# Patch projection, scan sums and gating products of a two-image Mamba-style block moved between engines

## Chip, cores and metric

The kernel runs on one NeuronCore of a Trainium2 chip, in one launch, in float32. The metric is the device time of one execution in microseconds (us), taken as the median of three runs. The engines are named as in the profile: PE is TensorE (the matrix engine), DVE is VectorE, ACT is ScalarE, POOL is GpSimd and SP is SyncE, which here only issues DMAs. PEld is the loading of weights into PE. PE writes to PSUM, a small memory beside the large SBUF.

## What is computed

Two images of 128 channels and 64 x 64 pixels pass two MetaFormer layers. Each layer has a token mixer and a mixture-of-experts network:

```
layer 0 mixer : four deformable convolutions (1x1, 1x1, 3x3, 7x7), a pooled branch, 1x1 fusion
layer 0 MLP   : top-2 of 8 experts
layer 1 mixer : h = LayerNorm(x); in_proj 128 -> 512 channels; depthwise 5x5 convolution
                x half (256): channel attention, causal conv1d of 4 taps, SiLU
                z half (256): position attention, SiLU
                dt = softplus(...); state[n] = exp(dt*A[n])*state[n] + dt*x*B[n]   (n = 0..15)
                y = (sum over n of C[n]*state[n] + D*x) * silu(z); out_proj 256 -> 128; residual
layer 1 MLP   : mixture of 64 experts
```

The change is in the layer 1 mixer. Its two matrix parts are linear, so the input projection may be done before or while the image is cut into patches, and the sum over n may be made in either orientation of the matrix.

## The kernel before

The order of every engine's instructions is written out by hand (`manual_schedule`). The long stages run in turn. Work that can go beside a stage is written as Python generators that yield; a `Side` object advances them by `step()`, so many steps per turn of the stage's loop. The order in which the Python program emits instructions is the order of each engine's queue.

1. **Sampling** (`L0Conv.sample`, L535): for each image, 8 groups of 60 taps, 480 turns of the loop. A turn gathers 4 x 128 rows of 2 KB by four indirect DMAs of POOL (L547), weights them on DVE (L558, L563, L564), transposes them on PE (L568), copies them on ACT (L577) and multiplies them on PE (L597). During the sampling of image 2, `rest` holds everything that image 1 needs up to its scan (`after(0)`: `finish`, the first MLP and `L1Conv.convs`). It is stepped 3 times per turn in the first group and 2 times in the others (L526).
2. **Scan** (`L1Conv.scan`, L1221): the sequence of each image is cut into 8 pieces of 512 positions. Of each piece there are 32 units: 16 states n by 2 halves of 128 channels; 512 units in all. A unit u is
   - POOL: `drive(u + 3)`, the product db = du * B of three units later (L1246)
   - ACT: the copy of the last unit's end state (L1310), then `decay(u + 2)`, da = exp(A*dt) into PSUM (L1253)
   - DVE: the scan, in place in da in PSUM (L1303), then the C product sc = da * C into SBUF (L1313)
   - PE: `add` of the last unit's sc to the accumulators py by four 128 x 128 identity transposes (L1271)
   - `side.step()` twice, which advances `prepare` of the next piece (L1118) and `project` of the last one (L1333)
   - during image 1, `rest.step()` five times, which advances `after(1)`, the same work for image 2 as in stage 1 for image 1.

   The rows of B and C are loaded, broadcast to 128 partitions, into `bcb`, 512 KB for each n, with 6 buffers (L1261). `rest` and `side` must be empty before the last units of a piece (L1292, L1305).
3. **Last MLP** (`L1Ffn.run`).

`L1Conv.convs` (L912) is where the patches are. `norm` (L1009) normalizes 512 tokens, transposes them and stores the normalized image `hd` to DRAM. Then, for each of four pairs of 64-channel blocks o, `strips` (L1024) loads `hd` again in 8 groups, projects it to 128 channels (one 128 x 128 by 512 matmul, L1032) and copies it by three ACT copies into `hs`, the image in overlapping strips. For each block o: 88 transposes cut 12 x 10 patches out of `hs` (L959) to give X; 64 matmuls with position matrices `tm` do the 5 x 5 convolution (L972) to give Y; and 48 transposes bring Y back to images of 64 channels (L988), stored by DMA. `copy` is an ACT copy of PSUM, `later` holds copies back by two steps. `channel_stats` and `channel_attention` follow block 3 and `position_attention` follows block 7.

`prepare` makes xs, zz (gated z), dt (`dl`), dt*x (`du`) and B, C (`bc`) of a piece, with a softplus polynomial whose first step is L1195 on DVE, and D*x (`dx`, L1217) on ACT. `project` copies py to SBUF (L1337), transposes it back (`pty`), multiplies it by zz (L1349), projects it (L1354), adds the residual and stores.

Of the kernel before, what the change touches and what calls it, by code (L numbers as in the profile page):

```python
# [176 lines left out]
class L0Conv:  # L177
# [279 lines left out]
    def run(self, build, after):  # L457
# [3 lines left out]
        with ExitStack() as ctx:  # L461
# [62 lines left out]
            for g in range(NG):  # L524
                nxt = self.load_group(1, g + 1) if g + 1 < NG else None
                self.sample(1, g, *cur, conv, rest, 2 if g else 3)  # L526
                cur = nxt
# [309 lines left out]
BCB = 6  # L837
# [31 lines left out]
class L1Conv:  # L869
# [3 lines left out]

    def __init__(self, env, dp, wp, x2, x3):
        nc, d = env.nc, env.d
        self.env, self.dp, self.x2, self.x3 = env, dp, x2, x3
        self.pos = dp.tile([512 // CG, KP, NPOS, CG], F32, name="pos")

        def load(name, shape, src=None):
            t = wp.tile(shape, F32, name="w_" + name)  # L880
            nc.sync.dma_start(out=t, in_=d[name] if src is None else src)
            return t

        self.wp = wp
        self.c1w = load("conv1d_w", [P, 2, 4])
        self.c1b = load("conv1d_b", [P, 2])
        self.xpw = load("x_proj_w", [P, 2, 40])
        self.dtb = load("dt_proj_b", [P, 2])
        self.A = load("A_log", [P, 2, DS])
        self.D = load("D", [P, 2])  # L890
        self.fc1 = load("ca_fc1_w", [P, 2, 16])
        self.fc2 = load("ca_fc2_w", [16, 256])
        self.saw = load("sa_conv_w", [14, 1])
        self.sqb = wp.tile([P, len(SQUARES)], F32, name="sqb")
        for i, (_, t, _) in enumerate(SQUARES):
            nc.vector.memset(self.sqb[:, i : i + 1], t)
        nc.scalar.activation(self.A, self.A, AF.Exp)
        nc.vector.tensor_scalar(self.A, self.A, -1.0, None, ALU.mult)
        self.xsd = [self.dp.tile([256, 3 + N], F32, name=f"xsd{b}", tag=f"xsd{b}") for b in range(B)]
        self.zsd = [self.dp.tile([256, N], F32, name=f"zsd{b}", tag=f"zsd{b}") for b in range(B)]  # L900
        self.hd = [self.dp.tile([P, N], F32, name=f"hd{b}", tag=f"hd{b}") for b in range(B)]
        self.att = [self.dp.tile([2, N + 6], F32, name=f"att{b}", tag=f"att{b}") for b in range(B)]
        self.sad = [self.dp.tile([1, N], F32, name=f"sad{b}", tag=f"sad{b}") for b in range(B)]
        self.w1 = [wp.tile([P, 2, 4], F32, name=f"w1_{b}") for b in range(B)]
        for b in range(B):
            for h in range(2):
                nc.sync.dma_start(out=self.xsd[b][h * P : (h + 1) * P, 0:3], in_=env.zero[:, 0:3])
            for s in range(2):
                nc.sync.dma_start(out=self.att[b][s : s + 1, 0:3], in_=env.zero[0:1, 0:3])
                nc.sync.dma_start(out=self.att[b][s : s + 1, N + 3 :], in_=env.zero[0:1, 0:3])  # L910

    def convs(self, b, sp, pp):  # L912
# [31 lines left out]
        yield from mixed([self.norm(b, g, sp, bank) for g in range(NG)], 2)  # L944
        zst = sp.tile([NPATCH, 2, 4, NPOS], F32, name="zst", bufs=1)
        for o in range(512 // CG):
            if o % 2 == 0:
                own = ipw[:, o * CG : (o + 2) * CG]
                yield from mixed([self.strips(b, g, own, hs, sp, bank) for g in range(NG)], 2)
# [4 lines left out]
            ch = slice(o % 2 * CG, (o % 2 + 1) * CG)  # L954
            for p0 in range(0, NPATCH, 8):
                ps = bank([KP, 8, CG], "ps1")
                for k in range(8):
                    i, j = divmod(p0 + k, NJ)
                    nc.tensor.transpose(  # L959
                        ps[:, k, :],  # L960
                        hs[ch, j, PH * i : PH * i + PH + 4, :].rearrange("p y x -> p (y x)"),
                        env.ident[ch, ch],
                    )
# [4 lines left out]
            Y = sp.tile([NPATCH, NPOS, CG], F32, name="Y", bufs=1)  # L968
            for c0 in range(0, CG, 8):
# [5 lines left out]
                later(copy(Y[:, :, c0 : c0 + 8], ps.rearrange("p c s -> p s c")))  # L975
                yield
            yield from last()

            x_half = o < 4
            for py in range(PH):  # L980
                img = sp.tile([CG, NI, W], F32, name="img", tag="io", bufs=3)
                ch = slice((o % 4) * CG, (o % 4 + 1) * CG)
                dst = self.xsd[b][ch, 3:] if x_half else self.zsd[b][ch, :]
                dst = dst.rearrange("c (i y x) -> c y i x", y=PH, x=W)[:, py, :, :]
                for x0, nx in ((0, 4), (4, 2)):
                    ps = bank([CG, nx, NPATCH], "ps3")
# [11 lines left out]
            if not x_half:  # L998
                nc.vector.tensor_reduce(zst[:, 0, o - 4, :], Y, AX.X, ALU.add)
                yield  # L1000
                nc.vector.tensor_reduce(zst[:, 1, o - 4, :], Y, AX.X, ALU.max)
# [7 lines left out]
    def norm(self, b, g, sp, bank):  # L1009
# [10 lines left out]
        nc.scalar.copy(hn, pb)  # L1020
        nc.scalar.dma_start(out=self.hd[b][:, g * 512 : (g + 1) * 512], in_=hn.rearrange("p j t -> p (j t)"))
        yield

    def strips(self, b, g, own, hs, sp, bank):  # L1024

        nc = self.env.nc
        h = sp.tile([P, 512], F32, name="h", tag="io", bufs=3)
        nc.sync.dma_start(out=h, in_=self.hd[b][:, g * 512 : (g + 1) * 512])
        for _ in range(3):
            yield  # L1030
        pb = bank([P, 8, W], "pj")
        nc.tensor.matmul(pb.rearrange("p y x -> p (y x)"), own, h, start=True, stop=True)  # L1032
        yield
# [84 lines left out]
    def prepare(self, b, k, sp, pp, res):  # L1118
# [9 lines left out]
        zz = sp.tile([P, 2, LC], F32, name="zc")  # L1128
        nc.sync.dma_start(out=zz, in_=self.zsd[b].rearrange("(h p) l -> p h l", p=P)[:, :, l0 : l0 + LC])
        xr = sp.tile([P, GT, C], F32, name="xr")  # L1130
        nc.sync.dma_start(out=xr, in_=self.x2[b][:, k * GT : (k + 1) * GT, :])
        sa = sp.tile([P, LC], F32, name="sab", bufs=1)
        nc.sync.dma_start(out=sa, in_=self.sad[b][0, l0 : l0 + LC].partition_broadcast(P))
# [4 lines left out]
        yield from gap(6)  # L1138

# [55 lines left out]
        nc.vector.tensor_scalar(q, e, LINEAR[0], LINEAR[1], ALU.mult, ALU.add)  # L1195
# [19 lines left out]
        dx = sp.tile([P, 2, LC], F32, name="dx", bufs=1)  # L1215
        for h in halves:
            nc.scalar.mul(dx[:, h, :], xs[:, h, :], self.D[:, h : h + 1])  # L1217
        res.update(dx=dx, zz=zz, dl=dl, du=du, xr=xr)
        yield

    def scan(self, sp, ps, pp, rest, ahead):  # L1221
# [4 lines left out]
        for state in states:  # L1226
            nc.vector.memset(state, 0.0)
        NK = N // LC
# [10 lines left out]
        pieces, das, dbs, bcb, tail = {0: res}, {}, {}, {}, iter(())  # L1239
# [23 lines left out]
        adds, py = deque(), []  # L1263

        def add(half, what, first, last):

            if first:
                py.append(ps.tile([P, GT, P], F32, name=f"py{half}", tag=f"py{half}", bufs=1))
            out = py[half]
            for j in range(GT):  # L1270
                nc.tensor.matmul(  # L1271
                    out[:, j, :],
                    what[:, j * P : (j + 1) * P],
                    env.ident,
                    is_transpose=True,
                    start=first and j == 0,
                    stop=last and j == GT - 1,
                )
# [6 lines left out]
        side, keep = Side(), None  # L1285
        for u, (k, n, half) in enumerate(units):
            now, i, state = pieces[k], u // 2, states[k // NK]
            if n == 0 and half == 0:
                side.add(tail)
# [13 lines left out]
            nc.vector.tensor_tensor_scan(s, s, dbs.pop(u), state[:, half, n : n + 1], ALU.mult, ALU.add)  # L1303
# [8 lines left out]
            sc = sp.tile([P, LC], F32, name="sc", bufs=5)  # L1312
            nc.vector.tensor_tensor(sc, s, bc[:, 1, :], ALU.mult)  # L1313
            keep = state[:, half, n : n + 1], s[:, LC - 1 : LC]
            for _ in range(2 if rest.todo or k != NK - 1 else 4):
                side.step()
            for _ in range(5):
                rest.step()

            while adds:  # L1320
                add(*adds.popleft())
            if n == 0 and half == 0:
                py.clear()
                adds.extend((h, now["dx"][:, h, :], True, False) for h in range(2))
            adds.append((half, sc, False, n == DS - 1))
            if n == DS - 1 and half == 1:
                add(*adds.popleft())
                yt = sp.tile([P, 2, GT, P], F32, name="yt", bufs=1)
                tail = self.project(k // NK, k % NK, tuple(py), yt, now["zz"], now["xr"], pp)
        for _ in tail:  # L1330
            pass

    def project(self, b, k, py, yt, ys, xr, pp):  # L1333

        env, nc = self.env, self.env.nc
        for half in range(2):
            nc.scalar.copy(yt[:, half, :, :], py[half])  # L1337
        yield
        yield
        pts = []  # L1340
        for half in range(2):
            pt = pp.tile([P, GT, P], F32, name="pty", tag="m")
            transpose4(nc, env.ident, pt, [yt[:, half, j, :] for j in range(GT)])
            pts.append(pt)
            yield
        yield
        for half in range(2):
            y = ys[:, half, :]
            nc.vector.tensor_tensor(y, y, pts[half].rearrange("p j t -> p (j t)"), ALU.mult)  # L1349
            yield  # L1350
# [368 lines left out]
```

## Time and profile before

| what | us |
|---|---|
| median of three runs | 8280.49 (8272.83 to 8282.75) |
| the profiled execution's own time | 8332.4 |
| its span, first instruction to last | 8330.6 |
| PE, PEld busy in it | 5808.5, 4000.1 |
| DVE, ACT, POOL busy in it | 5729.7, 2120.9, 4590.5 |
| mean granted PE clock | 0.8 |

Read against the units' first and last instructions in the trace, the sampling of image 1 runs to 3150 us, that of image 2 to 6038 us, the first piece is prepared alone until 6085 us, the scan of image 1 runs to 7436 us, that of image 2 to 8055 us, and the last MLP to the end.

In the rows of the profile, "busy" is the time an engine's instructions of a group cover, then comes the mean of one in ns, then the idle time just before them and what ended it. In a table of windows the number after x counts instructions. A row of the timeline gives the start, the length, the engine, the line, what is written and read, and how many equal instructions were merged.

### The profile page before, as it was taken

The numbers are of one execution on the slowest core, as the hardware profiler recorded it, in microseconds if no ns is written. First come the engines' busy times: TensorE is split into PE (matmuls) and PEld (weight loads), VectorE is DVE, ScalarE is ACT, GpSimd is POOL, SyncE is SP. The second block draws the span as 40 slices with busy tenths as digits, with TensorE's granted clock in tenths as the row PEclk, the third lists the DMA queues.
The fourth block names the chain that finished last, engine by engine and source line by source line (L and its number), as shares of the span: only waits on it lengthen the run. The fifth ranks groups of instructions, "written<-read, shape, count | busy, mean of one in ns | idle before, by whom it ended". The sixth has DMA issues, their size and how long they took to land. (4 is left out here: it accounts for less than half of the span.)

```text
span 8330.6 us, 83751 instructions
## 1 busy us (share of the span) xinstructions
PE 5808.5 (70%) x27808; PEld 4000.1 (48%) x27808; DVE 5729.7 (69%) x8508; ACT 2120.9 (25%) x4432; POOL 4590.5 (55%) x4576
## 2 busy tenths in 40 slices
PE   2688888888888867766766676666755565855558
PEld 2456656666666644443434443344434444733335
DVE  1577777777777776777786667666647745669981
ACT  1111111111111113211111221112163344655540
POOL 0456666666666666666666666666534433347640
PEclk7788999999999988888888888788876665656568
DMA  4677666666666668867677777777653344434434
GB/s 128 185 249 216 195 207 203 205 213 197 207 203 206 208 212 261 270 213 234 218 240 203 228 204 223 219 206 216 176 166 135 127 110 107 128 106 149 145 124 141
DMA packets 636007, 1579.35 MB, mean 190 GB/s; under 512 B 167700, under 2 KB 247356, under 8 KB 623036
## 3 DMA queue, kind: packets, MB, share of 16 engines
q0 software_dynamic: 307200, 1006.88, 40.6%
q1 hardware_dynamic: 298284, 515.10, 19.5%
q10 hardware_dynamic: 30096, 52.03, 1.7%
q8 instruction: 226, 3.70, 0.2%
q14 instruction: 201, 1.65, 0.1%
HBM read 1456.11 MB, written 120.01 MB: 189 GB/s over the span
## 5 line engine op out<-in xcount | busy, mean ns | idle before, releaser
L547 POOL DMA_INDIRECT v<-table,idx x3840 | 3643.7, 949 | 2384.2 <-issue 1000.0
L597 PE MATMUL out<-st,regw 128*128 128x512 f32 x3840 | 2115.3, 676 | 161.2 <-issue 108.7
L558 DVE TENSOR_TENSOR v<-v,pw 128x1024 f32<-128x1024 f32 x960 | 1169.5, 1218 | 1060.9 <-DMA v<-table,idx 871.0
L568 PE MATMUL pst<-ident,v 128*128 128x128 f32 x7680 | 1240.2, 304 | 823.3 <-issue 529.5
L577 ACT COPY st<-pst 128x512 f32<-128x512 f32 x960 | 558.3, 585 | 4347.3 <-remote 2367.5
L568 PEld LDWEIGHTS pst<-ident,v 128*128 128x128 f32 x7680 | 1001.1, 157 | 1162.1 <-issue 786.9
L564 DVE TENSOR_TENSOR v<-v,low 128x512 f32<-128x512 f32 x1920 | 1318.0, 686 | 65.4
L563 DVE TENSOR_TENSOR low<-v,pw 128x512 f32<-128x512 f32 x1920 | 1329.0, 692 | 33.4
L1246 POOL TENSOR_TENSOR db<-du,bcb 128x512 f32<-128x512 f32 x512 | 660.0, 1293 | 937.2 <-DVE da L1303 897.4
L597 PEld LDWEIGHTS out<-st,regw 128*128 128x128 f32 x3840 | 762.0, 221 | 776.6 <-issue 713.7
L334 PEld LDWEIGHTS po<-wout,ring 128*128 128x128 f32 x5120 | 740.1, 198 | 366.5 <-issue 365.1
L334 PE MATMUL po<-wout,ring 128*128 128x147 f32 x5120 | 785.6, 299 | 167.4 <-issue 162.3
L1303 DVE TENSOR_TENSOR_SCAN da<-da,state,db 128x512 f32<-128x512 f32 x512 | 657.1, 1283 | 278.3 <-ACT da L1253 260.8
L1271 PE MATMUL py<-ident,sc 128*128 128x128 f32 x2048 | 463.0, 379 | 336.2 <-DVE sc L1313 335.1
L1271 PEld LDWEIGHTS py<-ident,sc 128*128 128x128 f32 x2048 | 338.6, 196 | 476.8 <-DVE sc L1313 441.5
L1313 DVE TENSOR_TENSOR sc<-da,bcb 128x512 f32<-128x512 f32 x512 | 354.2, 692 | 48.6 <-DVE da L1303 1.9
L1253 ACT ACTIVATE da<-delta,w_A_log 128x512 f32<-128x512 f32 x512 | 354.0, 692 | 17.3 <-DVE delta L1209 1.5
L972 PE MATMUL ps<-tm,X 120*88 120x48 f32 x2048 | 246.1, 299 | 62.9 <-ACT Y L924 22.5
L972 PEld LDWEIGHTS ps<-tm,X 120*88 120x88 f32 x2048 | 241.7, 213 | 94.4 <-issue 41.4
L959 PE MATMUL ps<-ident,hs 64*120 64x64 f32 x1408 | 142.1, 271 | 124.9 <-ACT X L924 69.8
L988 PE MATMUL ps<-ident,Y 88*64 88x88 f32 x768 | 108.1, 291 | 155.9 <-ACT img L924 100.1
L959 PEld LDWEIGHTS ps<-ident,hs 64*120 64x120 f32 x1408 | 125.5, 177 | 184.2 <-ACT X L924 89.5
(270 smaller groups left out, 4811.1 us busy)
## 6 DMA issues: line engine op xcount, KB each, us to landing
bcb<-bc SPq DMA_DIRECT2D x256, 512.0 KB
regw<-in_regw SPq DMA_DIRECT2D x66, 1280.0 KB
v<-table,idx POOLq DMA_INDIRECT x3840
yd<-ys ACTq DMA_DIRECT2D x128, 256.0 KB
yc<-yd SPq DMA_DIRECT2D x32, 1024.0 KB
gb<-gd SPq DMA_DIRECT2D x16, 2048.0 KB
wt<-in_weight SPq DMA_DIRECT2D x32, 1024.0 KB
tm<-pos SPq DMA_DIRECT2D x16, 1440.0 KB
```

The lines of the kernel that those rows point to most:

```text
L334: m()
L547: nc.gpsimd.indirect_dma_start(out=v[:, j, :], out_offset=None, in_=self.table[b], in_offset=bass.IndirectOffsetOnAxis(ap=idx[:, j, t : t ...
L558: nc.vector.tensor_tensor(up, up, w, ALU.mult)
L563: nc.vector.tensor_tensor(low, v4[:, two, 2:4, :], w, ALU.mult)
L564: nc.vector.tensor_tensor(up[:, two], up[:, two], low, ALU.add)
L568: nc.tensor.matmul(pt[:, j, :], v4[:, j, q, :], env.ident, is_transpose=True, start=j == 0 and q == 0, stop=j == GT - 1 and q == 1,)
L577: nc.scalar.copy(st, pt.rearrange("p j t -> p (j t)"))
L597: nc.tensor.matmul(self.out[half], self.regw[t // CH][:, t % CH, half * P : (half + 1) * P], st, start=first, stop=last,)
L972: nc.tensor.matmul(ps[:, c, :], X[:, c0 + c, :], tm[:, :, c0 + c], start=True, stop=True)
L1246: nc.gpsimd.tensor_tensor(dbs[u], pieces[k]["du"][:, half, :], bcb[u // 2][:, 0, :], ALU.mult)
L1271: nc.tensor.matmul(out[:, j, :], what[:, j * P : (j + 1) * P], env.ident, is_transpose=True, start=first and j == 0, stop=last and j == GT ...
L1303: nc.vector.tensor_tensor_scan(s, s, dbs.pop(u), state[:, half, n : n + 1], ALU.mult, ALU.add)
```

## The change

- **Projected patches.** `hd`, `strips` and the projection in 512-token groups go. `norm` copies the transposed, not yet projected image straight into `hs` (three ACT copies, 8 groups, once per image). The 88 patch transposes of a block become 88 matmuls of the patch (128 channels x 120) by that block's 64 columns of the projection.
- **Image 2 only: one way back for two blocks.** Y holds 128 channels, and the 48 transposes back, their copies and DMAs are done for two blocks at once, with 128 partitions instead of 64.
- **Identity products.** `add` is one ordinary matmul by the identity (or by a diagonal matrix of D, for D*x) with 512 columns, not four transposes; py keeps [channel, position], so `project` reads py directly and `yt`, `pty` and `dx` go. The sums are added two units after their product (three for D*x) and not one. `project` starts two units later, ahead of `prepare`, and loads its residual itself.
- **Image 2: 9 of 32 C products by POOL.** In the units of `ASIDE` the scan writes to SBUF, and POOL multiplies one unit later, behind that unit's `drive`.
- L1195 goes to ACT; `bcb` has 5 buffers and is fetched one n later; `sc` has 6; `rest` is stepped 4 times a unit, not 5, and 2 times a turn in the first sampling group of image 2, not 3; the loads of z and of the position weights move behind six steps.

```diff
-                self.sample(1, g, *cur, conv, rest, 2 if g else 3)
+                self.sample(1, g, *cur, conv, rest, 2)
...
-BCB = 6
+BCB = 5
+ASIDE = (2, 5, 8, 11, 14, 17, 20, 23, 26)
...
+        yg = CG if b == 0 else 2 * CG
...
-            if o % 2 == 0:
-                own = ipw[:, o * CG : (o + 2) * CG]
-                yield from mixed([self.strips(b, g, own, hs, sp, bank) for g in range(NG)], 2)
...
+            own = ipw[:, o * CG : (o + 1) * CG]
...
-                    nc.tensor.transpose(
-                        ps[:, k, :],
-                        hs[ch, j, PH * i : PH * i + PH + 4, :].rearrange("p y x -> p (y x)"),
-                        env.ident[ch, ch],
-                    )
+                    patch = hs[:, j, PH * i : PH * i + PH + 4, :].rearrange("p y x -> p (y x)")
+                    nc.tensor.matmul(ps[:, k, :], patch, own, start=True, stop=True)
...
-        nc.vector.tensor_scalar(q, e, LINEAR[0], LINEAR[1], ALU.mult, ALU.add)
+        nc.scalar.activation(q, e, AF.Identity, bias=self.lin, scale=LINEAR[0])
...
-            for j in range(GT):
-                nc.tensor.matmul(
-                    out[:, j, :],
-                    what[:, j * P : (j + 1) * P],
-                    env.ident,
-                    is_transpose=True,
-                    start=first and j == 0,
-                    stop=last and j == GT - 1,
-                )
+            nc.tensor.matmul(py[k, half], by, what, start=first, stop=last)
...
-            nc.vector.tensor_tensor_scan(s, s, dbs.pop(u), state[:, half, n : n + 1], ALU.mult, ALU.add)
+            aside = k >= NK and u % (2 * DS) in ASIDE
+            sc = sp.tile([P, LC], F32, name="sc", bufs=6)
+            to = sc if aside else s
+            nc.vector.tensor_tensor_scan(to, s, dbs.pop(u), state[:, half, n : n + 1], ALU.mult, ALU.add)
...
-            sc = sp.tile([P, LC], F32, name="sc", bufs=5)
-            nc.vector.tensor_tensor(sc, s, bc[:, 1, :], ALU.mult)
-            keep = state[:, half, n : n + 1], s[:, LC - 1 : LC]
+
+            if lag:
+                nc.gpsimd.tensor_tensor(*lag, ALU.mult)
+                lag = None
+            if aside:
+                lag = sc, sc, bc[:, 1, :]
+            else:
+                nc.vector.tensor_tensor(sc, s, bc[:, 1, :], ALU.mult)
+            keep = state[:, half, n : n + 1], to[:, LC - 1 : LC]
...
-            for _ in range(5):
+            for _ in range(4):
                 rest.step()
...
-            nc.vector.tensor_tensor(y, y, pts[half].rearrange("p j t -> p (j t)"), ALU.mult)
-            yield
+            nc.vector.tensor_tensor(y, y, py[half], ALU.mult)
+            yield
+        yield
```

## The prediction

> **What bounds the kernel now.** I read the table of windows first, cut at the stages (sampling of image 2; preparing the first piece, left out here; scan of image 1 beside the fusion, MLP and norm of image 2; beside its patches; the rest of image 1's scan; seven of the eight pieces of image 2). Columns: window, its length, then busy time of PE, PEld, DVE, ACT, POOL, granted PE clock, DMA.
>
> ```profile
> core 0: us, PE busy (x) PEld busy (x) DVE busy (x) ACT busy (x) POOL busy (x), PEclk, DMA share, GB/s
> 3150.00:6040.00 2890.00, 1983.44 (x8978) 1222.17 (x8979) 2066.82 (x2962) 565.11 (x1150) 1801.85 (x1896) 0.83 0.73 222
> ...
> 6085.00:6695.00 610.00, 337.07 (x1595) 258.56 (x1595) 421.50 (x697) 287.47 (x532) 241.27 (x163) 0.68 0.41 140
> 6695.00:7322.00 627.00, 440.95 (x2826) 368.78 (x2825) 325.55 (x335) 316.35 (x707) 203.30 (x161) 0.62 0.43 111
> 7322.00:7436.00 114.00, 48.65 (x136) 21.71 (x136) 66.38 (x68) 57.29 (x93) 50.35 (x40) 0.53 0.28 88
> 7436.00:7989.00 553.00, 295.60 (x1176) 195.16 (x1176) 526.11 (x532) 316.53 (x609) 389.77 (x309) 0.61 0.43 148
> ```
>
> Only image 2's scan has a clear owner: DVE, 526 of 553 us. Image 1's scan (6085 to 7436, 1351 us) has none; there the queues wait for each other. The waits of its patch part show how (engine and line, what it waited for, us, times, longest):
>
> ```profile
> DVE da L1303 <- ACT da L1253: 209.2, 49, 18.6
> ACT Y L924 <- PE ps L972: 100.0, 43, 11.5
> ...
> ACT img L924 <- DMA xsd<-img: 42.5, 15, 4.6
> ```
>
> The scan waits for an exponential, which stands in ACT's queue behind a copy that waits for PE's patch matmuls, or for a store. So PE's time counts here. The groups give prices (busy, mean ns):
>
> ```profile
> L597 PE MATMUL out<-st,regw 128*128 128x512 f32 x3840 | 2115.3, 676 | 161.2 <-issue 108.7 <-ACT ys L611 44.4 <-ACT st L577 3.8
> ...
> L1246 POOL TENSOR_TENSOR db<-du,bcb 128x512 f32<-128x512 f32 x512 | 660.0, 1293 | 937.2 <-DVE da L1303 897.4 <-issue 22.1 <-DMA bcb<-bc 9.2
> ...
> L1303 DVE TENSOR_TENSOR_SCAN da<-da,state,db 128x512 f32<-128x512 f32 x512 | 657.1, 1283 | 278.3 <-ACT da L1253 260.8 <-ACT state L1310 10.9 <-POOL db L1246 4.6
> ...
> L1271 PE MATMUL py<-ident,sc 128*128 128x128 f32 x2048 | 463.0, 379 | 336.2 <-DVE sc L1313 335.1 <-DVE gf_v L125 0.3
> ...
> L1313 DVE TENSOR_TENSOR sc<-da,bcb 128x512 f32<-128x512 f32 x512 | 354.2, 692 | 48.6 <-DVE da L1303 1.9 <-issue 1.3 <-PE pfo L673 0.5
> ...
> L959 PE MATMUL ps<-ident,hs 64*120 64x64 f32 x1408 | 142.1, 271 | 124.9 <-ACT X L924 69.8 <-ACT hs L1039 24.9 <-issue 20.0
> ```
>
> Counts matter more than means. L597 is called twice in each of the 960 turns of the sampling loop, 1920 calls, and has 3840 records. An ordinary f32 matmul therefore runs as two passes. L1271 has 512 x 4 = 2048 records and L959 has 2 x 8 x 88 = 1408: a transpose is one. A pipelined record's mean holds latency; its pace is read in the timeline, at half clock and at full:
>
> ```profile
> 7634.93 1.12 PE L1271 MATMUL py<-ident,sc 128*128 128x128 f32 x4
> ...
> 7637.24 0.66 PE L1271 MATMUL py<-ident,sc 128*128 128x128 f32 x4
> ```
>
> Start to start, 128 columns take 0.109 us at full clock and 0.213 at half, 512 columns (from L597) 0.429 and 0.853, the 64 columns of L959 0.059 and 0.107, L972 0.085 and 0.147.
>
> **The change part by part.**
>
> *Identity products.* Four transposes were 0.44 us (full) or 0.85 (half). One matmul is two passes of 512: 0.86 or 1.71. The change doubles this; removing three of four instructions saves nothing. The Trainium skill (page TensorE: Matmul & The Clock Gate, section Terms) calls transpose mode four times faster for f32. By that the add would be 1.74 or 3.4 us, which would make PE the bound of image 2; the counts say two, and I take two. D*x goes from 8 transposes to 4 passes a piece, +0.9 to 1.7 us. Gone with them: 8 back transposes a piece (0.9 to 1.7 us), two copies of py (2 x 0.58, ACT) and dx (2 x 0.71, ACT). The same page of the Trainium skill (section Part 4: PE-mode transpose) says transposes do not count as activity that raises the clock. In this trace the scan of image 2, full of transposes, holds 0.61, while sampling, with 4 long passes in some 6 us, holds 0.83. If that is the cause, the new adds lift the clock; if not, half clock stays usual. My sum takes a clock between, a little above before.
>
> *Projected patches.* For image 2, beside the scan, the four strips rounds take 117 us (between neighbouring phases in the trace: 25, 38, 27, 27), 160 of some 1175 rest steps. They go; the copies into hs, now in norm, cost 8 x 1.2 us of ACT there. Each block's 88 transposes become 176 passes: +5.2 us (full) or +9.4 (half), times 8. These phases took 154 us; with the doubled adds of the units they span I put +50. The eight convolution phases (160 us), near PE's pace already, get +12. Four of eight ways back go: these phases took 175 us with the waits behind them (19 to 41 us each at half clock, 9 to 19 at full), so about -80. Channel statistics: +5. Patch part: -117 + 50 + 12 - 80 + 5 = -130.
>
> *Four rest steps a unit.* About 1175 - 160 - 80 + 8 = 943 steps are left, 236 units at 4; now 235 units at 5. The rest ends at the same unit, inside its cover of 252. But fusion, MLP and norm spread from 110 units over 137, and each further unit brings its own 1.98 us of DVE plus 0.45 of preparing where DVE is full (most of the 404 us of the MLP), less where ACT is: 27 x about 2.2 = +60. From 7322: the same, 0.
>
> *Sampling of image 2.* The turns of the sampling loop that carry strips (about 80, near 5.6 us) give way to bare ones near 5.6: nothing. 704 patch transposes become 1408 passes, +41 to 75 us of PE, in 44 turns of the loop. At full clock it hides below POOL's four issues (4 x 1.25 us); at half PE is already full in such a turn. I take +5, bounds -10 and +40. 152 fewer rest steps cover 60 fewer on offer, so nothing is left at the end.
>
> *POOL's products.* A piece takes 553/7 = 79 us; DVE is busy 526/7 = 75.2. Nine products less: -6.2. L1195 to ACT: -1.1 (ACT is at 57% here; its +1.06 hides). DVE: 67.9. POOL: 389.8/7 = 55.7 + 9 x 1.27 = 67.1. The scan of these units writes SBUF, which the trace doesn't show. It still reads one operand from PSUM, as does L1349, which writes SBUF at 0.68 and is unharmed by POOL; so 1.28 (bounds 1.17, its shortest, and 1.7). But the steps of the polynomial with both operands in SBUF (L1204) take 1.22 alone and about 1.72 beside POOL; a busier POOL makes some four more of them slow: +2. POOL bursts: in some 9 units, 10 products of prepare, 9 db and 3 C products, 22 x 1.25 = 27.5 us against DVE's 19; db is three units (4 to 6 us) ahead, so 3 to 4 us of new stall. Per piece 79 - 7.3 + 2 + 3 = 76: 7 x -3 = -21; the last piece, without prepare, -5. Queued behind a late C product are db and prepare's products; its add stands two units back on PE.
>
> *Others at nothing.* bcb with 5 buffers loses about 4 us of lead; its 512 KB land some 3 us after issue and are used some 12 us after that (never under 4), so the lead covers it; uncovered it costs the missing us per n. The moved loads of z and residual have 6 to 8 steps. The end: no copy and transposes back, -3.
>
> Sum: +5 - 130 + 60 - 21 - 5 - 3 = -94 against the execution's 8332.4, so 8238. That execution stands 52 us above the median; the same difference from 8280.5 gives 8186.
>
> **The rivals.** *PE at half clock* (ends slower): two passes everywhere, clock not lifted. In image 2 PE then needs 32 x 1.71 + 3.4 (D) + 10.2 (px, pd, po) = 68 us a piece in queue order, so with its waits some 81: +2 x 7. Patches: 8 x 9.4, and doubled adds, leave -85 of -130; adds in the front part +80 instead of +60; sampling +35; ends -3. Together about +40: 8320. It decides if the clock in the scans stays at or below 0.6. For it: long half-clock stretches at 6725 to 6810 during dense small matmuls. Against: 0.83 with long matmuls.
> *The clock rises* to 0.85 in the scans: patches -200, and less waiting in the front part: about -180 in all, 8100.
> *POOL becomes the bound of image 2*: the bursts eat the gain, 79 a piece stays: -73, so about 8210.
>
> **How the numbers follow.** The likeliest case, 8140 to 8235, gets 0.45; POOL as the bound, 0.15; the risen clock, 0.20; PE at half clock, 0.20, of which about a third ends within 0.2% (16.6 us, about what measurement can tell). Faster 0.79, same 0.07, slower 0.14. The range 8085 to 8290 leaves out the far halves of the last two clock cases.
>
> **What would show it.** PE records of py: 1088, each N = 512, two per add. PE clock from 7436 on: above 0.75 for the steps as summed, 0.6 for the slow rival. Pieces of image 2 at 76 us; DVE's share falling, POOL near 90%. Image 1's scan near 1280 us, with its patch part near 500 and its front near 670. Sampling of image 2 within 40 us of 2890. The forecast is wrong if the front of image 1's scan grows by over 120 us, if PE's queue holds ACT longer than now, or if the scan into SBUF is slowed by POOL.

## The result and the profile after

The changed kernel takes 8188.5 us in the median (8175.4 to 8198.4, 4 runs), the kernel before 8279.0 beside it (8272.8 to 8282.8): ratio 0.989, interval 0.9873 to 0.9908. The forecast was 8186. The profiled execution of after took 8175.4 us (span 8173.6). The two profiled spans differ by 157 us, the medians by 90. Some 72 us of the 157 lie ahead of the first scan, about half of them in image 1's sampling, whose code is the same. They are put down to the two executions: before's stands 52 us above its median, after's 13 below, and the variants below with after's sampling, on other chips, reach the first scan at 6050 to 6088 us (before 6085, after 6013). So only what follows from the first scan on, 85 us, is read as the change.

Line numbers of after: da L1245 (was L1253), db L1238 (L1246), scan L1292 (L1303), C product L1308 (L1313), GpSimd's C product L1303, add L1261 (L1271), q on ScalarE L1187 (L1195), q times e L1189 (L1197), later steps of the polynomial L1196 (L1204), fourth tap of the causal convolution L1151, patches L965 (L959), convolution L973 (L972), copies L927 (L924), position weights L1105 (L1112).

The table of windows of after (columns as before; the sampling of image 2, then the three parts of image 1's scan, then seven pieces of image 2):

```profile
core 0: us, PE busy (x) PEld busy (x) DVE busy (x) ACT busy (x) POOL busy (x), PEclk, DMA share, GB/s
3112.00:5965.00 2853.00, 2040.78 (x9636) 1315.28 (x9634) 2074.70 (x2972) 539.04 (x1070) 1808.44 (x1903) 0.84 0.72 223
...
6013.00:6665.00 652.00, 414.32 (x1424) 245.01 (x1425) 477.21 (x761) 322.83 (x611) 292.06 (x202) 0.75 0.43 145
6665.00:7191.00 526.00, 416.95 (x2890) 329.46 (x2889) 264.20 (x266) 222.99 (x458) 156.50 (x124) 0.81 0.37 96
7191.00:7285.00 94.00, 62.95 (x91) 16.32 (x90) 61.27 (x61) 59.43 (x97) 48.06 (x38) 0.71 0.32 108
7285.00:7842.00 557.00, 349.47 (x644) 132.84 (x643) 488.88 (x463) 304.86 (x587) 476.85 (x372) 0.78 0.43 146
```

The last part of image 1's scan begins here at the first matmul of the position weights (7190.8 us). In the prediction's table of before it begins at 7322, 23 us ahead of the same matmul (7345.2), so those two rows are not the same stages. Cut at the matmul, before reads:

```profile
6695.00:7345.00 650.00, 440.95 (x2826) 368.78 (x2825) 331.90 (x342) 317.64 (x708) 207.09 (x164) 0.62 0.42 108
7345.00:7436.00 91.00, 48.65 (x136) 21.71 (x136) 60.03 (x60) 56.01 (x92) 46.56 (x37) 0.52 0.32 104
```

Image 1's scan went from 1351 to 1272 us: front +42, patch part -124, rest +3. Seven pieces of image 2 went from 553 to 557: although VectorE's busy time fell from 526 to 489 us, nothing became faster there. The last piece is 7.7 us shorter (64.9 to 57.2), the end 1.8. The granted clock rose in every scan stage (0.61 to 0.78 in image 2).

The waits of after's patch part:

```profile
DVE da L1292 <- ACT da L1245: 156.6, 34, 12.4
ACT X L927 <- PE ps L965: 98.1, 62, 4.5
POOL db L1238 <- DMA bcb<-bc: 70.9, 8, 17.8
...
ACT Y L927 <- PE ps L973: 37.6, 30, 3.7
```

The scan's wait for the exponential fell from 209 to 157 us. ScalarE's copies of Y wait less for PE (38 us, before 100), those of X more (98, before 19). The row of bcb is new: with five buffers GpSimd waits for the data of db (9.2 us in image 1's whole scan before, 152 now).

The convolution phases of the patch part show the clock at work. Cut from the trace by the first matmul of each phase, the eight took 161 us before and 120 after. The granted clock in them was 0.5 in six of the eight before (0.87 and 0.95 in the others), and 1.0 in six of the eight after (0.97 and 0.82 in the others). The last one, before and then after:

```profile
7282.20:7303.50 21.30, 21.30 (x140) 21.21 (x141) 4.00 (x5) 5.37 (x14) 3.15 (x3) 0.50 0.01 3
```

```profile
7130.70:7144.20 13.50, 13.50 (x136) 11.95 (x136) 4.90 (x6) 5.36 (x13) 3.83 (x3) 1.00 0.01 1
```

Groups of the seven pieces of image 2 after, kept apart by form:

```profile
L1261 PE MATMUL py<-sc,ident 128*128 128x512 f32 x448 | 273.3, 750 | 175.3 <-POOL sc L1303 153.4 <-DVE sc L1308 21.9
...
L1303 POOL TENSOR_TENSOR sc<-sc,bcb 128x512 f32<-128x512 f32 x63 | 82.8, 1315 | 1.5 <-ACT state L1299 1.5
L1292 DVE TENSOR_TENSOR_SCAN sc<-da,state,db 128x512 f32<-128x512 f32 x63 | 80.4, 1275 | 4.0 <-ACT state L1299 3.2
...
L1189 DVE TENSOR_TENSOR q<-q,e 128x1024 f32<-128x1024 f32 x7 | 23.7, 3382 | 20.7 <-ACT q L1187 20.7
```

448 records for 224 adds: two passes each, as taken. The scan into SBUF costs 1.275 us, the same as into PSUM (1.279). The last row is the surprise: VectorE's product of q and e takes 3.38 us and waits 3.0 us for q each time. Before, it took 1.36 us:

```profile
L1197 DVE TENSOR_TENSOR q<-q,e 128x1024 f32<-128x1024 f32 x7 | 9.5, 1360 | 0.2
```

### The profile page after: what moved, and what is told of

The parts are those of the page before. It is cut to its first block, busy times and chain, and to the rows that moved or that the text cites. A ratio compares the mean times of both kernels' runs of the same rounds, so it can differ in the third digit from the quotient of the medians.

```text
span 8173.6 us, 83001 instructions
## 1 busy us (share of the span) xinstructions
PE 5968.5 (73%) x27680; PEld 3971.5 (49%) x27680; DVE 5675.7 (69%) x8419; ACT 2024.5 (25%) x4158; POOL 4689.4 (57%) x4648
## 5 line engine op out<-in xcount | busy, mean ns | idle before, releaser
L597 PE MATMUL out<-st,regw 128*128 128x512 f32 x3840 | 2073.2, 665 | 129.5 <-issue 87.5
L1238 POOL TENSOR_TENSOR db<-du,bcb 128x512 f32<-128x512 f32 x512 | 670.7, 1317 | 738.9 <-DVE da L1292 551.0
L1261 PE MATMUL py<-sc,ident 128*128 128x512 f32 x1024 | 637.5, 750 | 251.0 <-POOL sc L1303 164.8
L1292 DVE TENSOR_TENSOR_SCAN da<-da,state,db 128x512 f32<-128x512 f32 x440 | 563.8, 1281 | 248.0 <-ACT da L1245 229.7
L1261 PEld LDWEIGHTS py<-sc,ident 128*128 128x128 f32 x1024 | 213.5, 231 | 554.4 <-POOL sc L1303 216.4
L965 PEld LDWEIGHTS ps<-ipw,hs 128*120 128x120 f32 x2816 | 351.7, 207 | 85.3 <-issue 43.0
L965 PE MATMUL ps<-ipw,hs 128*120 128x64 f32 x2816 | 350.8, 289 | 38.4 <-ACT X L927 23.7
L1245 ACT ACTIVATE da<-delta,w_A_log 128x512 f32<-128x512 f32 x512 | 353.5, 691 | 18.3 <-DVE delta L1201 2.8
L1308 DVE TENSOR_TENSOR sc<-da,bcb 128x512 f32<-128x512 f32 x440 | 304.3, 692 | 44.0 <-PE py L1261 4.6
L973 PEld LDWEIGHTS ps<-tm,X 120*88 120x88 f32 x2048 | 188.5, 170 | 57.3 <-ACT Y L927 26.4
L973 PE MATMUL ps<-tm,X 120*88 120x48 f32 x2048 | 192.6, 267 | 21.3 <-ACT Y L927 14.4
L673 PE MATMUL pfo<-yc,fw 128*128 128x256 f32 x512 | 144.7, 422 | 78.4 <-ACT yc L675 72.2
```

The costliest lines, as they stand in the source:

```text
L597: nc.tensor.matmul(self.out[half], self.regw[t // CH][:, t % CH, half * P : (half + 1) * P], st, start=first, stop=last,)
L965: nc.tensor.matmul(ps[:, k, :], patch, own, start=True, stop=True)
L1238: nc.gpsimd.tensor_tensor(dbs[u], pieces[k]["du"][:, half, :], bcb[u // 2][:, 0, :], ALU.mult)
L1261: nc.tensor.matmul(py[k, half], by, what, start=first, stop=last)
L1292: nc.vector.tensor_tensor_scan(to, s, dbs.pop(u), state[:, half, n : n + 1], ALU.mult, ALU.add)
```

## The experiments

The theory after the result had two parts. (1) The whole gain comes through image 1's scan: less work in `rest` lets it be handed out four steps a unit, so that more units lie beside it and fewer stand bare after it. (2) GpSimd's products in image 2 gain nothing, because VectorE loses beside them what it saves. Rivals: the gain comes from the smaller work as such, or from the clock, or from bcb; and image 2 is held by the move of q to ScalarE.

**Image 2: which of the two moves costs.** First, no C product on GpSimd:

```diff
-ASIDE = (2, 5, 8, 11, 14, 17, 20, 23, 26)
+ASIDE = ()
```

> The changed kernel, but all 32 C products of a piece stay on DVE. In the changed kernel a piece of image 2 takes 79.6 us against 79.0 before, although DVE has 5.2 us less to do. Theory A (two new waits share the loss: DVE waits some 3 us for the polynomial's first step on ACT and the next product is locked out of SBUF by POOL for 2 us; and POOL's extra products make DVE wait some 4 us for its adds and for db): without the POOL products a piece gains their waits and loses their 6.2 us, so 79 to 82 us, time 8185 to 8210. Theory B (POOL is simply the bound of image 2, and the move to ACT costs nothing): with POOL relieved, DVE's 75.2 - 1.5 and its old waits give 77.5 us, time about 8172.

Measured: ratio 0.9888 (0.9861 to 0.9915), image 1's scan 1271.8; 78.2 to 78.5 us a piece, between the two theories (79 to 82, 77.5), the last 64.5. Second, q back on VectorE, the nine products kept:

```diff
-        nc.scalar.activation(q, e, AF.Identity, bias=self.lin, scale=LINEAR[0])
+        nc.vector.tensor_scalar(q, e, LINEAR[0], LINEAR[1], ALU.mult, ALU.add)
```

> The changed kernel, but the polynomial's first step is on DVE again. Theory A: the wait for ACT (3.0 us a piece) and part of the lock (2.0) go and 1.5 us of work come back: a piece of image 2 at 76 to 77 us, time 8160 to 8170. Theory B (POOL is the bound): the piece stays at 79 to 80 us and the time at 8185 to 8190.

Measured: 0.9871 (0.9844 to 0.9898), image 1's scan 1254, pieces 80.3, so A is wrong; the last 57.2. The product of q and e has its own price again (1.225 us), but now q itself, on VectorE, takes 5.2:

```profile
L1187 DVE TENSOR_SCALAR q<-e 128x1024 f32<-128x1024 f32 x7 | 36.6, 5222 | 4.0 <-ACT e L1185 4.0
```

Third, both undone:

> The changed kernel with neither POOL products nor the move to ACT. Both theories: image 2's pieces at 79 us as in the kernel before, since the identity products lie beside DVE; the clock stays near 0.78 if the long matmuls are what raises it. Image 1 is unchanged but for the first step, so the time is 8180 to 8190. If the identity products as two passes cost image 2 something, the piece is above 80 us.

Measured: 0.9886 (0.9854 to 0.9917), scan 1271, pieces 78.5, the last 64.5; q on VectorE takes 1.19 us, and VectorE has next to no waits.

Against 79.6 in the changed kernel, the nine products cost about 1.2 us a piece (1.8 with q on VectorE) and give 7.3 us only in the last piece, where nothing is prepared. Moving q is worth 0.7 us beside the products and nothing without them. The ratios do not separate these four kernels, since image 1's scan varies by 18 us between them; the pieces do, each repeating within 0.3 us. So the move of q is cleared as the cause, and a gain without the wait for q (76 to 77) was not there: with q on VectorE the lock, below, only met another instruction.

**The products only where nothing is prepared.**

```diff
-            aside = k >= NK and u % (2 * DS) in ASIDE
+            aside = k == B * NK - 1 and u % (2 * DS) in ASIDE
```

> The changed kernel with POOL's products in the last piece only, where no next piece is prepared. From the runs without them (78.4 us a piece, last 64.5) and with them (79.6, last 57.2): seven pieces at 78.4 and the last at 57.2, so image 2's scan is 606 us against 614, and the kernel 8 us faster than the changed one, hardly above what can be told.

Measured: 0.9894 (0.9876 to 0.9912), scan 1283, no gain over the changed kernel; pieces 79.5, 79.1, 82.3, 82.3, 78.4, 78.5, 78.5, the last 57.5. The last piece's gain stays; two pieces stand out by 4 us, which comes back below.

**Image 1's scan: five steps again.**

```diff
-            for _ in range(4):
+            for _ in range(5):
                 rest.step()
```

> The changed kernel with 5 rest steps a unit in image 1, as before. Theory A (a unit costs its 2 us and more wherever it stands): the front part of image 1's scan shrinks from 652 us to 605 to 620, but some 45 more units stand bare after the rest, so the image-1 scan stays within 20 us of 1272 and the time within 20 us of 8188. Theory C (spreading over more units was a pure loss of some 40 us): the image-1 scan near 1230, the time near 8150. Theory D (spreading pays, as units hide the rest's waits): the image-1 scan above 1295, the time above 8210.

Measured: 0.9991 (0.9978 to 1.0004), no change at all, with every other edit in. Image 1's scan took 1384 us, as D has it (above 1295). Its windows (front, patch part, rest of the scan):

```profile
6088.00:6715.00 627.00, 372.80 (x1345) 221.56 (x1346) 395.62 (x700) 298.15 (x553) 239.68 (x168) 0.75 0.40 133
6715.00:7264.00 549.00, 431.74 (x2834) 357.74 (x2834) 221.04 (x220) 203.34 (x411) 126.53 (x100) 0.73 0.33 83
7264.00:7471.00 207.00, 143.41 (x224) 43.63 (x224) 161.89 (x166) 112.90 (x205) 120.35 (x96) 0.70 0.35 116
```

The front has 112 units here and 138 in the changed kernel, for 627 and 652 us: 26 more units cost 25 us. The patch part has 71 units here and 91 there, for 549 and 526 us: 20 more units cost nothing. The bare stretch has 73 units here and 27 there, for 207 and 94 us: 2.5 us for each of the 46. So the front and the patch part last as long as the chain of `rest` (PE, ScalarE's copies, DMA), and units beside it are nearly free. The scan waits longer for its exponential as well, in that run's patch part:

```profile
DVE da L1292 <- ACT da L1245: 214.3, 35, 15.6
```

214 us against 157. The removed rounds alone, in other words, only shorten the cover under which units ride (the patch part from 650 us with 121 units to 549 with 71); the pacing turns them into time. Nor does a higher clock alone bring the gain: over image 1's scan it is 0.73 here against 0.64 before, and nothing is gained.

**One step finer.** If that is so, three steps beside every eighth unit should gain again.

```diff
-            for _ in range(4):
+            for _ in range(4 if u % 8 else 3):
```

> The changed kernel with three steps of the rest beside every eighth unit and four beside the others. Theory A, units beside the rest are nearly free and bare units after it cost about 2.4 us each: the rest ends some 7 units later (unit 237 in place of 230), image 1's scan takes about 1272 - 16 = 1256, ratio 0.987. Theory B, each unit costs its 2 us wherever it stands: 1272 +- 3, ratio 0.989. Image 2's pieces stay at 79.6.

Measured: 0.9857 (0.9836 to 0.9879). `rest` ends at unit 236 instead of 229; image 1's scan took 1260, 11 us less than in the changed kernel, where A expected 16 and B none. The sign fits A, but the kernels in which nothing that runs in image 1's scan was edited (the changed kernel, the ones without products, with products in the last piece only, and with five of them, below) lie between 1253 and 1283, so this one difference is within their spread.

**Identity products alone**, on the kernel before (with the new `project`, the moved loads and six sc buffers; six bcb buffers, five steps, old convolutions, q on VectorE):

```diff
-            adds.append((half, sc, False, n == DS - 1))
+            adds.append((u + 2, k, half, env.ident, sc, False, n == DS - 1))
```

> The kernel before with the identity products alone (adds as one matmul of two passes, two units late; project reads the sums directly; D*x by a diagonal matrix), 5 rest steps, 6 bcb buffers, first step on DVE, strips as before. The rest needs its 1175 steps as before, so this shows what the adds do by themselves. Theory A (the lifted clock pays for the doubled passes): the clock in image 2's pieces rises from 0.61 to 0.75 or more, the pieces stay within 1 us of 79.0, and image 1's scan stays within 25 us of 1351; ratio 0.993 to 1.003. Theory B (PE's doubled passes cost where PE is waited for): image 1's scan longer than 1380, ratio above 1.003. Theory C (the gain of the whole change comes from here, by the higher clock and adds that no longer hold PE's queue): image 1's scan under 1310, ratio below 0.993.

Measured: 1.0021 (1.0013 to 1.0029), about as A has it. Image 1's scan +24 (1375), pieces of image 2 78.5 (-0.5) but for the first (80.4). The clock went from 0.61 to 0.74 in image 2 and from 0.64 to 0.70 in image 1's scan. So the longer adds do lift the clock without the patch edits, but not in the patch part, where it went from 0.62 to 0.64 only (0.81 in the changed kernel):

```profile
6680.00:7358.00 678.00, 510.16 (x2529) 335.83 (x2528) 326.88 (x337) 302.33 (x683) 201.12 (x160) 0.64 0.40 103
```

Its eight convolution phases took 181 us, six of them at 0.5. The full clock there came only in the kernels that project the patches by ordinary matmuls, just ahead of each of these phases (the five-step run is one: 137 us). The doubled passes of the adds are 256 x 0.42 = 108 us of PE in image 1's scan even at full clock; the scan shows 24, so the rest is hidden or paid by the clock (which of the two, this run does not say). Beside the five-step run (1384 with the patch edits, and with five bcb buffers) it also says that removing strips and four ways back brought nothing to the scan at five steps a unit.

**Two ways back for two blocks**, as before:

```diff
-        yg = CG if b == 0 else 2 * CG
+        yg = CG
```

> The changed kernel, but image 2's blocks go back one by one with 64 partitions, as before and as image 1's. About 80 more rest steps, which end at about unit 253, at the edge of their cover. Theory A (a way back costs some 15 to 20 us beside the scan, as the forecast took): image 1's scan is 60 to 80 us longer, 1330 to 1350. Theory B (its steps ride in the shade of other waits): at most 30 us longer.

Measured: 0.9918 (0.9896 to 0.994), scan 1301, 29 us more, as B has it, and 18 above the spread just named. The phases of the way back, each up to the next phase and with the channel statistics, took 212 us instead of 164.

**Six bcb buffers.** To make room for the sixth, sc has four buffers here, and no product is on GpSimd; the kernel to compare with is that of the first experiment:

```diff
-BCB = 5
-ASIDE = (2, 5, 8, 11, 14, 17, 20, 23, 26)
+BCB = 6
+ASIDE = ()
...
-            sc = sp.tile([P, LC], F32, name="sc", bufs=6)
+            sc = sp.tile([P, LC], F32, name="sc", bufs=4)
```

> The changed kernel without POOL products, with 6 bcb buffers and one n more of lead as before (and 4 instead of 6 sc buffers, for the room). In the changed kernel POOL waits 71 us in the patch part of image 1's scan for bcb loads, before 9 us in the whole scan. If that wait is on the path, image 1's scan loses 30 to 70 us against 1272 of the same kernel with 5 buffers, and the time falls below 8225 on a chip like the last one. If the scan there waits for ACT anyway, as the waits of DVE say, the image-1 scan stays within 10 us.

Measured: 0.9957 (0.9943 to 0.9972), scan 1298, pieces 82.0. GpSimd's wait for bcb fell from 158 us (first experiment) to 11.5, and the scan was not shorter but 26 us longer. VectorE now waits for sc buffers, which PE's adds give back late: 376 us in image 1's scan, while its wait for the exponential fell from 221 to 19, and 3.8 us a piece in image 2. Inconclusive: four sc buffers cost more than the sixth bcb could show. Six bcb buffers with all else unchanged were not tried, nor the patch edits alone on the kernel before. Nor was the slower pace alone: there 1175 steps at four a unit would need 294 units, and the cover is 252.

**Where the products stand.** Five products in units without preparing on GpSimd:

```diff
-ASIDE = (2, 5, 8, 11, 14, 17, 20, 23, 26)
+ASIDE = (0, 3, 25, 27, 29)
```

> The changed kernel with GpSimd's C products of image 2 in five units of each piece in place of nine: units 0, 3, 25, 27 and 29, where the preparing of the next piece asks nothing of GpSimd and gives VectorE no step with two SBUF operands. Image 1's scan is untouched (1272). Theory A, the place decides: each product takes 0.69 us from VectorE and delays nothing, so a piece takes 78.5 (measured without any product) less 3.5, thus 75, the last one 61, and the ratio is 0.985. Theory B, a product gains nothing wherever it stands, since the add or the GpSimd db behind it comes late: 78.5 to 79.6 a piece, ratio 0.989.

Measured: 0.9875 (0.9846 to 0.9904), scan 1253. Three pieces took 75.0 us, as A has it, four 78.3; the last 60.7. The three are the last of the seven; why two levels, comes below. The product L1189 is back to its own price:

```profile
L1189 DVE TENSOR_TENSOR q<-q,e 128x1024 f32<-128x1024 f32 x7 | 8.6, 1225 | 24.5 <-ACT q L1187 24.5
```

**Longer distances instead**, with all nine products:

```diff
             nc.gpsimd.tensor_tensor(zz[:, h, :], zz[:, h, :], sa, ALU.mult)
-            yield
+            yield from gap(2)
...
         nc.scalar.activation(q, e, AF.Identity, bias=self.lin, scale=LINEAR[0])
-        yield
+        yield from gap(3)
```

> The changed kernel with two more steps of preparing between ScalarE's q and VectorE's product of q with e, and one more between GpSimd's products of xs and VectorE's fourth tap; nine products stay. Theory A, the two new waits of VectorE (3.0 and 2.4 us a piece) come of short distances in the hand-written order: they go, a piece takes 74 to 75.5, ratio 0.985. Theory B, GpSimd is behind with its queue in units 7 to 22 whatever the distances: the waits come back at the scan (for db) and at later steps, 78 to 79.6 a piece, ratio 0.988 to 0.989. The last piece (57.2) and image 1's scan (1272) stay.

Measured: 0.9866 (0.9835 to 0.9897), scan 1248, pieces 80.1, so A is wrong: the wait for q is gone (0), and the same product now takes 5.94 us. The timeline of one piece shows why (PE, ScalarE and DMA left out):

```profile
7455.27 1.26 POOL L1303 TENSOR_TENSOR sc<-sc,bcb 128x512 f32<-128x512 f32 x1
...
7455.69 1.29 DVE L1292 TENSOR_TENSOR_SCAN da<-da,state,db 128x512 f32<-128x512 f32 x1 [1.53 <-ACT state L1299]
...
7456.50 3.72 POOL L1238 TENSOR_TENSOR db<-du,bcb 128x512 f32<-128x512 f32 x3
...
7457.68 6.06 DVE L1189 TENSOR_TENSOR q<-q,e 128x1024 f32<-128x1024 f32 x1
7460.18 1.26 POOL L1303 TENSOR_TENSOR sc<-sc,bcb 128x512 f32<-128x512 f32 x1
7461.40 1.26 POOL L1238 TENSOR_TENSOR db<-du,bcb 128x512 f32<-128x512 f32 x1
7463.67 1.28 DVE L1292 TENSOR_TENSOR_SCAN da<-da,state,db 128x512 f32<-128x512 f32 x1
```

GpSimd works without a gap until 7462.7, here since 7421. VectorE's product, with all operands in SBUF, starts at 7457.7 and ends at 7463.7, that is 1.1 us after GpSimd's last, its own 1.22: it got in only once GpSimd stopped. The Trainium skill (page SBUF — State Buffer, section Who interferes with whom) has the two share a port pair as an exclusive lock; the trace agrees. The scan, with an operand in PSUM, is not touched (1.29 us beside GpSimd in the second row shown), nor is the C product (0.69).

How long the lock lasts depends on VectorE's instruction. In the first seven pieces of image 2 of all fourteen profiles (before, after and twelve variants), the product of q and e began 35 times while a gapless run of GpSimd still had instructions to come, and each time it ended 1.1 us after the end of that run. The `scalar_tensor_tensor` steps, with all operands in SBUF too, began so 230 times and each time ended before the run did, in at most 1.9 us; GpSimd then took up to 2.3 us for its next instruction instead of 1.26. One in the same run of GpSimd as above:

```profile
7433.99 1.26 POOL L1148 TENSOR_TENSOR zc<-zc,sab 128x512 f32<-128x512 f32 x1
...
7434.06 1.74 DVE L1151 SCALAR_TENSOR_TENSOR xs<-xc,w,xs 128x512 f32<-128x512 f32 x1 [1.19 <-POOL xs L1143]
...
7435.21 1.72 POOL L1238 TENSOR_TENSOR db<-du,bcb 128x512 f32<-128x512 f32 x1
```

q as a `tensor_scalar` on VectorE waited for the end of the run like the product (10 of 11 times). A kernel with the product written as `scalar_tensor_tensor` was not run.

**Together**: products in free units, all nine in the last piece, the longer distance ahead of L1189, the finer pacing.

```diff
-ASIDE = (2, 5, 8, 11, 14, 17, 20, 23, 26)
+ASIDE = (0, 3, 26, 28, 30), (2, 5, 8, 11, 14, 17, 20, 23, 26)
...
-        yield
+        yield from gap(3)
...
-            aside = k >= NK and u % (2 * DS) in ASIDE
+            aside = k >= NK and u % (2 * DS) in ASIDE[k == B * NK - 1]
...
-            for _ in range(4):
+            for _ in range(4 if u % 8 else 3):
```

> The changed kernel with what the last three runs point to: GpSimd's products in units 0, 3, 26, 28 and 30 of a piece, all nine in the last piece; two more steps between ScalarE's q and VectorE's product; three rest steps beside every eighth unit. Theory A: the wait for q (1.7 us in the better pieces of the run with five products, 4.9 in the others, whenever PE hands over the second input of the softplus late) is hidden by the longer distance and, with GpSimd's products out of the way, no lock takes its place: 73.3 to 74 a piece, the last 57.3, image 1's scan 1260, ratio 0.981 to 0.983. Theory B: VectorE then waits for ScalarE or PE one step further on: 75 to 78 a piece, ratio 0.985.

Measured: 8171.1 against 8297.7 beside it, 0.9841 (0.9817 to 0.9865), the fastest of all; its interval lies below that of the changed kernel (from 0.9873). Image 1's scan took 1266. Pieces: 77.0, 74.1, 73.8, 77.0, 74.3, 74.1, 77.0, the last 57.5. Again two levels, with one and the same code. PE's timeline of a short piece and of the long one after it, at the same place (pd feeds the softplus):

```profile
7501.27 1.13 PE L1261 MATMUL py<-sc,ident 128*128 128x512 f32 x2
7502.33 1.12 PE L1176 MATMUL pd<-xd,dtw 8*128 8x512 f32 x2
```

```profile
7575.21 2.08 PE L1261 MATMUL py<-sc,ident 128*128 128x512 f32 x2
7577.21 2.07 PE L1176 MATMUL pd<-xd,dtw 8*128 8x512 f32 x2
```

Two passes take 2.07 us in the long piece, 1.12 in the short one. The granted clock in these few us, first short, then long:

```profile
7501.00:7505.00 4.00, 4.00 (x9) 1.18 (x8) 3.81 (x5) 2.99 (x7) 4.00 (x4) 1.00 0.35 83
```

```profile
7575.00:7581.00 6.00, 6.00 (x7) 1.50 (x6) 5.70 (x7) 2.86 (x6) 6.00 (x6) 0.50 0.50 139
```

ScalarE, which reads pd next, waits 2.4 and 2.5 us for it instead of 0.3 and 0.5, what follows in its queue is late, and VectorE stands still for 3.1 us at the scan. In this kernel, in the one with five products and in the one with products in the last piece only, each of the nine long pieces has both pd at half clock, and none of the twelve short ones has. The one long piece of the identity products alone (80.4) has it too. The piece's mean clock does not tell (0.78 in the long piece shown, 0.77 in the short one): what counts is the clock in those few us.

## Why the prediction was right

The total was right, within 3 us of the median, and image 1's scan was foreseen well: -70 stood for it, -79 came. Image 2's gain did not come, and errors cancelled: -18 in the front against +9 in the rest of image 1's scan and, with the last piece and the end, +23 in image 2. From the first scan on, -94 less the +5 of the sampling stood as -99; the trace has -85. That this lands within 3 us is in part luck.

- **Identity products, two passes.** Right: 1088 records, 512 columns each. The four-times rule would have given 2048 + 128. The clock rose, from 0.61 to 0.74 in image 2 without the patch edits. That fits what the Trainium skill (page TensorE: Matmul & The Clock Gate, section Part 4: PE-mode transpose) says of transposes, but PE was also busy for longer (372 us against 296 in seven pieces), and no run separates the two.
- **Patch part, -130.** It became -124 by errors that cancel. Patches +51 (taken +50). The strips went with 82 us, not 117: from the first matmul of a round to the first patch it is 82, and the 117 also held waits behind ways back, which were in the 175 of those as well. Ways back with the channel statistics -60 (taken -80 and +5), and only 29 us on the scan when undone. The convolutions, taken as "near PE's pace already" and at +12, became 40 us shorter: their pace was that of half clock, and the projected patches ahead of them come with the full one.
- **Front, +60.** It became +42, which is 1.5 us for each of 28 units. The step "each further unit brings its own 1.98 us of DVE" failed: the five-step run shows 0.96 us a unit in the front and nothing in the patch part. The front is not VectorE's; units fill gaps in the chain of `rest`.
- **The same end unit, "from 7322: the same".** Right: the position weights begin at unit 229 and before at 230, and from there it is 94 us for 91. That four steps a unit keep the end there turned out to be the edit on which the whole gain hangs, as the five-step run shows; the prediction had it as a cost only.
- **GpSimd's products, -21.** This step failed: +4. (Its own sum, 79 - 7.3 + 2 + 3, is 76.7 and not 76, so -16.) The third rival, "the bursts eat the gain, 79 a piece stays", has the right time and the right place, with another mechanism. GpSimd is busy 477 of 557 us, 86 %, so it is not full. In its dense stretch (units 5 to 19 of a piece, 30 instructions in 37.7 us) its run without a gap locks out VectorE's product of q and e. The term "some four more of them slow: +2" was this lock, sized by the 1.72 us of a single overlap; behind a run the product took up to 6.1. Five products out of that stretch give 75.0 where the clock is full at pd, which is 0.7 us saved for each.
- **L1195 to ScalarE, -1.1.** 0.7 beside the products, nothing without them. "Its +1.06 hides" failed in the order of one queue: VectorE waits 3.0 us for it.
- **bcb with five buffers at nothing.** The lead was not enough in image 1's scan (152 us of GpSimd's waiting). Whether any of it reaches the end stays open.
- **The slow-clock rival** did not come as a state of a whole stage (0.71 to 0.86 in the scans), but a small form of it did in four of the variants: 2 to 4 us in a piece whose pd meets the half clock.

## What to carry to other kernels

Where background work is dealt out in steps beside a loop, removing part of it may gain nothing until it is dealt out more slowly, so that it still covers the loop to its end: look at what the loop costs beside it (here 0 to 1 us a unit) and after it (2.5). Work moved from VectorE to GpSimd must be put where GpSimd has gaps, or where VectorE has no `tensor_tensor` or `tensor_scalar` with all operands in SBUF; the sum of busy times doesn't show that, the timeline of one period does. Two tables of windows are compared only when both are cut at the same instruction. And a piece with two lengths under the same code asks for the clock at one place, not for its mean.

## What was not expected of the hardware

- A VectorE product of 1024 columns, 1.22 us alone, took 3.4 us on average in the changed kernel, 5.9 with the longer distances, and there it ended 1.1 us after the end of a gapless run of GpSimd instructions. q as a `tensor_scalar` on VectorE went from 1.19 to 5.2. A `scalar_tensor_tensor` in the same run took 1.74 and came in between two GpSimd instructions.
- The granted clock in image 2 rose from 0.61 to 0.74 when the adds by transposes became ordinary matmuls of twice the passes. In the convolution phases of the patch part it stayed at 0.5 in six of eight then, and was 1.0 in six of eight with the projected patches.
- The two passes of one pd matmul took 1.12 us in one piece and 2.07 in the next, with the same instructions ahead of them.
